# Third group's correlation in its own products, set-aside copies on GpSimd, last windows copied by ScalarE

## The chip, the cores and the metric

The kernel runs on one core of one Trainium2 chip. The metric is the device time of one execution in microseconds (us). The core has a matrix engine (TensorE, "PE" in the profile, with its weight loads listed apart as "PEld"), VectorE ("DVE"), ScalarE ("ACT"), GpSimd ("POOL"), and SyncE ("SP"), which here issues nearly all DMAs. Each engine works through its own instructions in order, and they wait for each other by semaphores.

## The reference

The input is a batch of 8 images with 768 channels of 32 x 32 pixels in float32. There are two layers, each with a residual:

```python
def _gn(v, G=32, eps=1e-5):
    g = v.reshape(B_, G, C_ // G, H_, W_)
    m = jnp.mean(g, axis=(2, 3, 4), keepdims=True)
    s = jnp.var(g, axis=(2, 3, 4), keepdims=True)
    return ((g - m) / jnp.sqrt(s + eps)).reshape(v.shape)
...
# layer 0: attention over 1024 tokens, 12 heads of 64; scores from variances of v and k
scores = var_v @ jnp.swapaxes(var_k, -2, -1) * scale
out = (softmax(scores) @ v) ... @ W_proj.T + b_proj
x = x + attention(_gn(x))
# layer 1: 1x1 convolution of the feature and of 28 correlation channels
feat_n = feature / norm
corr = [sum_c(feat_pad[:, :, r:h+r, cc:w+cc] * feat_n) for r, cc in offsets]   # 28 shifts
out = einsum('bchw,oc->bohw', concatenate([feature, corr]), conv_w) + conv_b
x = x + conv(_gn(x))
```

So the convolution has two parts: a 768 x 768 product over the 1024 pixels, and a product of the 28 correlation channels with a 768 x 28 matrix. The second is what the change moves.

## The kernel before, in words

**Products.** The large products (keys and values, projection "p", convolution "c") are done in seven block products instead of eight, numbered p = 1 to 7. For projection and convolution there are three groups g = 0, 1, 2. A group holds the output channel blocks g and g + 3, each 128 channels, for two token halves of 512 each. One block product is a "unit": three pairs of (128 x 128 weights, 128 x 512 operand), and `halves` (line 347) splits each pair into two matmul calls of 64 output columns. So a unit has six calls. In the trace each call is two records: the 3072 records of line 800 are 8 images x 6 head pairs x 8 tiles x 4 calls = 1536 calls. The products accumulate in a PSUM bank "x" (p = 1, 6, 7, 4 in turn), "y" (5, 3) or "z" (2). After p = 1, 5, 6 VectorE adds the partial sum to the output tile `acc`, and after p = 2, 3, 7, 4 one output block is final (`Wide.take`, line 1064).

**Correlation.** For each image `Corr` (line 1119) turns the image into blocks (`turn`), multiplies them on TensorE ("grams", `gram`, line 1138, 8 of them), copies each result out of PSUM into one of the `win` tiles, sends it to DRAM ("windowed"), reads diagonals back ("dd"), scales them, sends rows to DRAM and gathers them. `product` (line 1239) then forms the 28 rows of `cs` on VectorE. Three DMAs copy them to partitions 32, 64 and 96 (line 1243). The weights `wcorr_sb` are copied likewise (line 488).

**Where the correlation goes into the convolution.** `Conv.more` (line 1281) names the units whose bank is then final: p in (2, 3, 7, 4). Such a unit is begun but not closed (`Wide.unit`, line 1038). Then `join` (line 1053) issues one matmul of 28 rows x 128 columns for each held unit, each on its own quarter of the partitions. Images 0 to 5 join first four, four (groups 0 and 1), then two and two (group 2). Image 6 joins by two throughout, six times. Image 7 has `apart`: 12 correlation products in banks of their own, two for each of six `corr` calls (line 1337), added by VectorE.

**The order of the work.** The emitter keeps a model clock (`Clock`, line 92) with a cost for each unit (`T_US`, `CORR_US`, `STEP_US`). It decides with it in what order instructions go onto each engine's list; the engines then run by semaphores alone. `work_off` (line 1374) mixes the units in `rest` with the attention of the next image, four steps of products at a time, each step needing two exponentials from ScalarE. If only work of cost 0 is left in `rest`, `work_off` passes time until attention is done (`TAIL`, line 1383). The conv of image b runs beside the attention of image b + 1. `project` (line 1397) follows.

**The end.** Image 6's units (0, 2) and (1, 2) are held back into image 7's projection (line 1452), so that TensorE has work while image 7 is normalised. Their operands and outputs are copied aside first: `set_aside` (line 1315), five ScalarE copies of 128 x 512 into three tiles of the exponentials' pool `expool` (six tiles). It stands before the last three units of `rest` for image 6. Then the last iteration runs two units of image 7's convolution, the 8 grams, 16 more units, and three times two `corr` calls and a unit.

**The start.** `keep_warm(WARM)` issues 31 small matmuls while the first image loads.

**Queues.** SP issues the weight loads of the units (line 337, seven tiles ahead), the image loads and stores, and all small transfers of the correlation, in emission order. An SP instruction whose tile is not free holds those behind it.

Of the kernel before, what the change touches and what calls it, by code (L numbers as in the profile page):

```python
# [8 lines left out]
ALU = mybir.AluOpType  # L9
# [4 lines left out]
P = 128  # L14
NB, C, H, W = 8, 768, 32, 32
N = H * W
J = C // P
# [33 lines left out]
KVBLOCKS = 5  # L51
TBLOCKS = 7
HELD = 12
TAIL = 0.0
EXP, SUM, STEP_US = 1.07, 1.15, 1.73
KV_US, T_US, CORR_US = 1.93, 2.58, 1.2
GRAM_US = 1.4
WARM, BRIDGE = 31, (3, 7)

# [19 lines left out]

def conv_order(b):

    return QUADS if b < NB - 2 else (PAIR[:-2] if b == NB - 2 else PAIR) + SINGLE


def windows(ap, *dims):
# [85 lines left out]
def two_layers(ctx, tc, x, wkv, wproj, bproj, wconv, wcorr, bconv, out):  # L173
# [301 lines left out]
    def load_corr_weights():  # L475

        zero = cs[0:NROW, 0, 0:PAD]
        for r in rows:
            nc.sync.dma_start(out=r[:, 0:PAD], in_=zero)
            nc.sync.dma_start(out=r[:, PAD + N : ROW], in_=zero)  # L480
        for line, step in enumerate(STEP):
            for j in (1, 2, 3):
                n, k = CHANNELS.index(step * j), 3 * line + j - 1
                nc.sync.dma_start(out=wcorr_sb[n : n + 1, :, :], in_=wcorr[k : k + 1, :, :])
                nc.sync.dma_start(out=wcorr_sb[NS + n : NS + n + 1, :, :], in_=wcorr[NS + k : NS + k + 1, :, :])
        nc.sync.dma_start(out=wcorr_sb[2 * NS : NCH, :, :], in_=wcorr[2 * NS : NCH, :, :])
        for n in range(1, 4):
            nc.sync.dma_start(out=wcorr_sb[n * FOUR : n * FOUR + NCH, :, :], in_=wcorr_sb[0:NCH, :, :])

    later.after(130.0, mask_rows)  # L490
    later.after(150.0, load_corr_weights)
# [445 lines left out]
    class Attention:  # L937
# [32 lines left out]
        def exp_work(self, pair, t):  # L970
            def may():
                if ("c", 1) not in pair.rows_at or self.made - self.done >= AHEAD or self.made - self.summed > LAG:
                    return None
                free = self.free_at[self.made - AHEAD] if self.made >= AHEAD else 0.0
                return max(pair.rows_at["c", 1], free)

            def job():
                pair.exponentials(t)
                self.made += 1
                self.exp_at = clock.act  # L980

            clock.act_work(2 * EXP, may, job)
# [46 lines left out]
    class Wide:  # L1029
# [8 lines left out]
        def unit(self, g, p, between=None):  # L1038
            w = t_stream.take(self.kind, g, p)
            pairs = [(w[:, k, :], self.operand(p, k)) for k in range(JH)]  # L1040
            taken = lambda ps: self.take(g, p, ps)
            more = self.more(g, p) if self.more else None
            if more is None:
                banks.product(g, p, T_US, HF, pairs, taken, self.home if g == 2 else None)
            else:
                apart = (g, p) == (0, 2) and self.joined[:1] == [4]
                self.held.append((*banks.begin(g, p, HF, pairs, stop=False, between=between, apart=apart), taken, *more))
                if len(self.held) == (self.joined[0] if self.joined else 2):
                    self.joined = self.joined[1:]
                    self.join()  # L1050
            t_stream.fill()
# [67 lines left out]
    class Corr:  # L1119
# [18 lines left out]
        def gram(self, t):  # L1138

            b = self.b  # L1140
            tall = min(TALL, H - 4 * t)
            n = tall * WIDE
            if t not in self.turned:
                self.turn(t)
            block = self.turned[t]
            ps = other([P, SPAN], f"gr{b}_{t}")
            for j in range(J):
                image = self.f[:, j, :].rearrange("p (y x) -> p y x", x=W)
                for side in range(2):
                    left = side * (HW - 3)  # L1150
                    nc.tensor.matmul(  # L1151
                        ps[side * HD : (side + 1) * HD, :n].rearrange("p (y x) -> p y x", x=WIDE),
                        lhsT=block[:, j, side, :],
                        rhs=image[:, 4 * t : 4 * t + tall, left : left + WIDE],
                        start=j == 0, stop=j == J - 1,
                    )
            for ahead in range(t + 1, min(t + (3 if b == NB - 1 else 2), MT)):
                if ahead not in self.turned:
                    self.turn(ahead)

            def out():
                win = wins[t % 2 if t < MT - 1 else 2]
                vector.tensor_copy(win[:, :n], ps[:, :n])
                for side in range(2):
                    to = windowed[b % 2][t : t + 1, side * (HD * PITCH + HD - 3) :]
                    nc.sync.dma_start(
                        out=windows(to, (HW * PITCH - 3, 4), (PITCH, HW), (1, WIN)), in_=win[side * HD : (side + 1) * HD, :]
                    )
                if t % 4 == 3:
                    later.after(4.0, lambda: self.diagonals(t // 4))  # L1170

            later.after(GRAM_US + 0.25, out)
# [50 lines left out]
        def gather(self):  # L1223
# [19 lines left out]
                    nc.sync.dma_start(out=cs[n * FOUR : n * FOUR + NCH, :, :], in_=cs[0:NCH, :, :])  # L1243
                later.after_dve(6.0, lambda: ready.add(("cs", b)))

            later.after(18.0, product)

    class Conv:


        def __init__(self, b, f, acc, after):
            self.b, self.f, self.acc, self.after = b, f, acc, after
            self.early, self.then = False, None
            self.turn = False
# [12 lines left out]
        def start(self):  # L1267
# [9 lines left out]
            self.wide.joined = [4, 4] if self.b < NB - 2 else []  # L1277
            ready.add(("acc", self.b))
            later.after(7.0, self.thirds)

        def more(self, g, p):


            if p not in (2, 3, 7, 4) or self.apart:
                return None
            return g + JH * (p in (7, 4)), {2: 0, 3: 1, 7: 1, 4: 2}[p]

# [7 lines left out]
            ready.add(("fourth", self.b))  # L1295

        def units(self):
            b, held, sizes = self.b, 0, [4, 4] if self.b < NB - 2 else []
            need = {7: (("third", b),), 4: (("fourth", b),)}
            out = []  # L1300
            for g, p in conv_order(b):
                keys, us = need.get(p, ()), T_US
                if self.more(g, p):
# [27 lines left out]

        def corr_units(self):
            return [
                (CORR_US, (("cs", self.b),), lambda n=n: self.corr(self.apart[n : n + 2])) for n in range(0, len(self.apart), 2)
            ]

        def corr(self, parts):

            self.turn = not self.turn
            av = None if self.turn else two_banks(f"av{self.b}_{parts[0][0]}")  # L1340
            for n, (i, hf) in enumerate(parts):
                at = slice(n * FOUR, n * FOUR + NCH)
                ps = other([P, HF], f"cc{self.b}_{i}_{hf}") if av is None else av[n]
# [30 lines left out]
    def work_off(rest, attention=None, beside=()):  # L1374
        while rest or (attention and not attention.over()):
            if attention and not attention.over():
                clock.feed_act()
                if attention.can_run():
                    next_to(beside)
                    attention.run()  # L1380
                    next_to(beside)
                    continue
                if ("v", attention.b, 1) in ready and sum(r[0] for r in rest) <= TAIL:
                    clock.pass_time(0.5)
                    continue
            if rest and ready.issuperset(rest[0][1]):
                us, _, unit = rest.pop(0)
# [130 lines left out]
    for b in range(NB + 1):  # L1518
# [8 lines left out]
        if b:  # L1527
# [17 lines left out]
            if b < NB:  # L1545
# [69 lines left out]
```

## Time and profile before

| what | us |
|---|---|
| runs of before | 2604.48, 2602.58, 2604.71 (median 2604.48) |
| the profiled execution | 2601.92 |
| its span in the profile | 2599.4 |
| outside the span | 2.5 |
| TensorE busy | 2586.6 (100% of the span) |
| VectorE, ScalarE, GpSimd busy | 1609.8, 1368.6, 416.0 |
| granted TensorE clock | 1.0 |

The page has shares of busy time, a row of 40 slices, and a chain followed back from the last instruction. The chain of waits says at each step what released the work. The timelines list merged runs of instructions of one engine: start, length, engine, line, operation, operands, count, and in brackets the idle time before it and who ended it. A table by windows gives the busy time of each engine within a stretch. Matmul ends are modelled, so rates of TensorE are read from starts.

### The profile page before, as it was taken

How to read it: one execution, taken by the hardware profiler on the slowest of the kernel's cores; microseconds unless marked ns; L12 is line 12 of the kernel's file. 1: busy time of each engine (PE TensorE's matmuls, PEld its weight loads, DVE VectorE, ACT ScalarE, POOL GpSimd, SP SyncE). 2: the span in 40 equal slices, each digit the busy share in tenths (PEclk: the TensorE clock that was granted, in tenths of full speed). 3: DMA queues.
4: the chain of work that ended last, by engine and by line, in shares of the span. 5: the costliest groups of instructions: out<-in, count | busy, mean ns of one | idle time of the engine just before them, and what ended most of it. 6: DMA issues, size and time to landing. Idle time of an engine off the chain costs nothing.

```text
span 2599.4 us, 40526 instructions
## 1 busy us (share of the span) xinstructions
PE 2586.6 (100%) x14776; PEld 1351.1 (52%) x14776; DVE 1609.8 (62%) x4118; ACT 1368.6 (53%) x1841; POOL 416.0 (16%) x444
## 2 busy tenths in 40 slices
PE   9999999999999999999999999999999999999999
PEld 5654465434664347643476435764356643575333
DVE  6868735775347853488535885357853578535764
ACT  1497179701797017970189701896018960199500
POOL 4320130004300043000330013300133001330000
PEclk9999999999999999999999999999999999999999
DMA  8866366355563655636556365463654636545323
GB/s 295 291 222 216 105 206 206 102 200 168 175 206 96 203 169 173 202 105 200 171 170 201 121 200 169 156 205 118 206 170 144 207 123 205 187 125 169 114 91 106
DMA packets 324716, 448.16 MB, mean 172 GB/s; under 512 B 59810, under 2 KB 245522, under 8 KB 324518
## 3 DMA queue, kind: packets, MB, share of 16 engines
q1 hardware_dynamic: 322454, 442.24, 53.0%
q10 hardware_dynamic: 2064, 3.34, 0.4%
q8 instruction: 117, 1.92, 0.3%
q14 instruction: 81, 0.66, 0.1%
HBM read 376.70 MB, written 64.40 MB: 170 GB/s over the span
## 4 chain that ended last, share of the span: by engine, by line
PE 96%; DVE 1%; DMA 1%; ACT 0%; issue 0%; POOL 0%; SPq 0%; DVEq 0%; ACTq 0%; POOLq 0%
PE x L350 34%; PE av L800 25%; PE y L350 17%; PE z L350 9%; PE own L350 5%; PE gr L1151 3%; PE den L831 1%; PE den L887 1%; PE y L1057 1%; PE z L1057 1%; ACT ex L774 0%; DMA bc<-vdr 0%; DVE acc L167 0%; DMA xn<-in_x_dram 0%; DVE bn L167 0%
## 5 line engine op out<-in xcount | busy, mean ns | idle before, releaser
L774 ACT ACTIVATE ex<-bc,nk 128x1024 f32<-128x1024 f32 x768 | 827.5, 1137 | 403.9 <-DMA bc<-vdr 206.1
L800 PE MATMUL av<-ex,v 128*64 128x512 f32 x3072 | 693.5, 593 | 1.2 <-ACT ex L774 1.1
L800 PEld LDWEIGHTS av<-ex,v 128*64 128x64 f32 x3072 | 332.2, 137 | 318.4 <-issue 199.3
L784 ACT ACTIVATE junk<-bk,vm 128x1024 bf16<-128x1024 f32 x368 | 420.4, 1142 | 28.8 <-DMA bk<-kdr 19.1
L167 DVE TENSOR_TENSOR acc<-acc,ex 128x1024 f32<-128x1024 f32 x300 | 345.2, 1211 | 0.8 <-ACT ex L774 0.8
L229 ACT COPY kp<-x 128x384 f32<-128x384 f32 x28 | 13.3, 478 | 524.1 <-PE x L350 515.4
L350 PE MATMUL y<-kv,s 128*64 128x384 f32 x1488 | 265.3, 487 | 0.3 <-POOL s L636 0.3
L350 PE MATMUL x<-kv,xn 128*64 128x384 f32 x1512 | 259.5, 486 | 0.0
L350 PE MATMUL x<-kv,s 128*64 128x384 f32 x1488 | 256.4, 486 | 0.0
L350 PEld LDWEIGHTS x<-kv,xn 128*64 128x64 f32 x1512 | 139.5, 137 | 104.0 <-issue 83.8
L350 PEld LDWEIGHTS x<-kv,s 128*64 128x64 f32 x1488 | 142.6, 137 | 93.3 <-issue 72.7
L350 PEld LDWEIGHTS y<-kv,s 128*64 128x64 f32 x1488 | 137.0, 137 | 89.9 <-issue 72.4
L530 POOL TENSOR_TENSOR rstda<-vea,neghalf 128x1 f32<-128x1 f32 x8 | 4.8, 595 | 958.6 <-DVE vea L167 958.6
L1136 POOL TENSOR_TENSOR turn<-f,ones 128x384 f32<-128x384 f32 x112 | 110.9, 1010 | 242.7 <-PE gr L1151 165.7
L350 PE MATMUL z<-kv,xn 128*64 128x384 f32 x768 | 133.7, 486 | 0.0
L350 PE MATMUL x<-f,wt 128*64 128x512 f32 x504 | 118.3, 592 | 0.0
L167 DVE TENSOR_TENSOR v<-y,v 128x128 f32<-128x128 f32 x180 | 40.9, 282 | 122.2 <-PE y L350 122.2
L636 POOL TENSOR_TENSOR s<-xn 128x384 f32<-128x384 f32 x64 | 65.6, 1035 | 304.3 <-PE x L350 190.0
L167 DVE BATCH_NORM_STATS2 vbn<-v 128x6 f32<-128x64 f32 x720 | 101.6, 209 | 0.0
L350 PEld LDWEIGHTS z<-kv,xn 128*64 128x64 f32 x768 | 74.9, 137 | 47.3 <-issue 36.6
L167 DVE SCALAR_TENSOR_TENSOR xn<-x,bconv_sb,xn 128x512 f32<-128x512 f32 x63 | 46.3, 745 | 80.8 <-PE x L350 79.7
L1151 PEld LDWEIGHTS gr<-f,turn 128*64 128x64 f32 x1344 | 87.8, 136 | 13.0 <-issue 4.8
(202 smaller groups left out, 3132.3 us busy)
## 6 DMA issues: line engine op xcount, KB each, us to landing
kv<-kvs SPq DMA_DIRECT2D x124, 576.0 KB
kv<-in_wkv_dram SPq DMA_DIRECT2D x95, 576.0 KB
bc<-vdr SPq DMA_DIRECT2D x96, 512.0 KB
f<-in_x_dram SPq DMA_DIRECT2D x48, 512.0 KB
bk<-kdr SPq DMA_DIRECT2D x46, 512.0 KB
x1d<-f SPq DMA_DIRECT2D x42, 512.0 KB
xn<-x1d SPq DMA_DIRECT2D x42, 512.0 KB
out_dram<-xn SPq DMA_DIRECT2D x82, 256.0 KB
```

What stands on the lines that cost most here:

```text
L167: return getattr(self.engine, name)(*args, **kw)
L229: nc.scalar.copy(to, at)
L350: nc.tensor.matmul(out[at], lhsT=lhsT[:, at], rhs=rhs, start=start, stop=stop, **kw)
L636: nc.gpsimd.tensor_tensor(self.sums[g][:, 0], a[g][2], a[g][3], ALU.add)
L774: nc.scalar.activation(ex, self.bc[e], AF.Exp, scale=self.kv.nk[self.half][:, h, t : t + 1])
L784: nc.scalar.activation(junk, self.bk[e], AF.Exp, scale=self.kv.m2[self.half][:, h, t : t + 1], accum_out=self.sums[:, e, t : t + 1],)
L800: nc.tensor.matmul(self.av[hf][e * HD : (e + 1) * HD, :], lhsT=self.vt[:, t, e, :], rhs=exs[e][:, hf * HF : (hf + 1) * HF], start=t == 0, ...
L831: nc.tensor.matmul(den[at * 32 : (at + 1) * 32, :], lhsT=ones[:, 0:32], rhs=self.acc[e][:, hf * HF : (hf + 1) * HF], start=True, stop=True,)
L887: nc.tensor.matmul(den[e * HD : (e + 1) * HD, :], lhsT=ones, rhs=self.acc[e][:, at], start=True, stop=True)
L1057: nc.tensor.matmul(t, lhsT=wcorr_sb[at, i, :], rhs=cs[at, tokens, :], start=False, stop=True, skip_group_check=True)
L1136: nc.gpsimd.tensor_tensor(to[:, :, side], half, windows(ones, ones.ap[0], (0, J), (HW, 4), (1, HW)), ALU.mult)
L1151: nc.tensor.matmul(ps[side * HD : (side + 1) * HD, :n].rearrange("p (y x) -> p y x", x=WIDE), lhsT=block[:, j, side, :], rhs=image[:, 4 * ...
```

## The change

- Units of group 2 take their correlation as a fourth pair within their own product: all 128 rows of `wcorr_sb` and of `cs`, through `halves`. For this the weights of blocks 2 and 5 are no longer copied to the other three quarters (rows 28 and up of these two blocks stay zero); the copies of the rest take six DMAs instead of three.
- Image 6 joins once four (groups 0 and 1), then two, then (in the projection) two; its order has the units (2, 5) and (2, 1) between the pairs. Image 7's `apart` has 8 parts instead of 12, four for each of two `corr` calls, and its last four units follow them. In the order of the emission the correlation must be there one unit earlier.
- `set_aside` copies on GpSimd (multiplication by ones) and stands at the end of `rest`, after all exponentials of image 7 have been emitted. `TAIL` goes.
- Image 7's window copies move from VectorE to ScalarE, and its `product` is emitted 12 us of model time after the gather instead of 18.
- 42 small matmuls at the start instead of 31.

```diff
-TAIL = 0.0
-KV_US, T_US, CORR_US = 1.93, 2.58, 1.2
+KV_US, T_US, CORR_US, OWN_US = 1.93, 2.58, 1.2, 0.43
-WARM, BRIDGE = 31, (3, 7)
+WARM, BRIDGE = 42, (3, 7)
...
-    return QUADS if b < NB - 2 else (PAIR[:-2] if b == NB - 2 else PAIR) + SINGLE
+    if b < NB - 2:
+        return QUADS
+    if b == NB - 2:
+        return PAIR[:10] + ((2, 5),) + PAIR[10:12] + ((2, 1),) + SINGLE[2:]
+    return PAIR + SINGLE
...
         for n in range(1, 4):
-            nc.sync.dma_start(out=wcorr_sb[n * FOUR : n * FOUR + NCH, :, :], in_=wcorr_sb[0:NCH, :, :])
+            for g in range(0, J, JH):
+                at = slice(g, g + JH - 1)
+                nc.sync.dma_start(out=wcorr_sb[n * FOUR : n * FOUR + NCH, at, :], in_=wcorr_sb[0:NCH, at, :])
...
                 self.made += 1
+                if self.made == HP * MT:
+                    ready.add(("made", self.b))
...
-            if more is None:
+            if more and g == JH - 1:
+                i, tokens = more
+                pairs.append((wcorr_sb[:, i, :], cs[:, tokens, :]))
+                banks.product(g, p, T_US + OWN_US, HF, pairs, taken)
+            elif more is None:
...
-                vector.tensor_copy(win[:, :n], ps[:, :n])
+                if b < NB - 1:
+                    vector.tensor_copy(win[:, :n], ps[:, :n])
+                else:
+                    act_copy(0.3, win[:, :n], ps[:, :n])
...
-            later.after(18.0, product)
+            later.after(18.0 if b < NB - 1 else 12.0, product)
...
-            self.apart = [] if b < NB - 1 else [(i, hf) for i in (0, 3, 1, 4, 2, 5) for hf in range(2)]
+            self.apart = [] if b < NB - 1 else [(i, hf) for i in (0, 3, 1, 4) for hf in range(2)]
+        def sizes(self):
+            return [4, 4] if self.b < NB - 2 else [4]
...
-            if p not in (2, 3, 7, 4) or self.apart:
+            if p not in (2, 3, 7, 4) or (self.apart and g < JH - 1):
                 return None
...
+            def copy(to, at):
+                one = windows(ones, ones.ap[0], (0, HF // HD), (1, HD))
+                to, at = [a.rearrange("p (n d) -> p n d", d=HD) for a in (to, at)]
+                nc.gpsimd.tensor_tensor(to, at, one, ALU.mult)
             for k in range(JH):
-                act_copy(0.55, self.high[k], self.f[:, JH + k, :HF])
+                copy(self.high[k], self.f[:, JH + k, :HF])
             for g in range(2):
-                act_copy(0.55, self.low[g], self.acc[:, g, :HF])
+                copy(self.low[g], self.acc[:, g, :HF])
...
-            self.turn = not self.turn
-            av = None if self.turn else two_banks(f"av{self.b}_{parts[0][0]}")
-            for n, (i, hf) in enumerate(parts):
+            some = [other([P, HF], f"cc{self.b}_{i}_{hf}") for i, hf in parts[:2]]
+            for n, (ps, (i, hf)) in enumerate(zip(some + two_banks(f"av{self.b}_{parts[0][0]}"), parts)):
...
-                if ("v", attention.b, 1) in ready and sum(r[0] for r in rest) <= TAIL:
-                    clock.pass_time(0.5)
-                    continue
...
-                    rest.insert(len(rest) - 3, (0.0, (), conv.set_aside))
+                    rest.append((0.0, (("made", b),), conv.set_aside))
             else:
                 units, parts = conv.units(), conv.corr_units()
-                rest += [first, start] + units[:2] + grams + units[2:18]
-                for n, unit in enumerate(units[18:]):
-                    rest += parts[2 * n : 2 * n + 2] + [unit]
+                rest += [first, start] + units[:2] + grams + units[2:17]
+                for n, unit in enumerate(units[17:]):
+                    rest += parts[n : n + 1] + [unit]
```

More of the change, by code (lines that the diff above doesn't have):

```diff
@@ L1253, in __init__ @@
             self.early, self.then = False, None
-            self.turn = False
-            self.apart = [] if b < NB - 1 else [(i, hf) for i in (0, 3, 1, 4, 2, 5) for hf in range(2)]
+            self.apart = [] if b < NB - 1 else [(i, hf) for i in (0, 3, 1, 4) for hf in range(2)]
             self.parts = {(i, hf, "f") for i in range(J) for hf in range(2)} | {(*q, "c") for q in self.apart}
             self.sums = TokenSums(f"f{b}", [f[:, k, :] for k in range(JH)], [f[:, JH + k, :] for k in range(JH)])
+        def sizes(self):
+            return [4, 4] if self.b < NB - 2 else [4]
         def residual(self, n):
@@ L1276, in start @@
             )
-            self.wide.joined = [4, 4] if self.b < NB - 2 else []
+            self.wide.joined = self.sizes()
             ready.add(("acc", self.b))
@@ L1297, in units @@
         def units(self):
-            b, held, sizes = self.b, 0, [4, 4] if self.b < NB - 2 else []
+            b, held, sizes = self.b, 0, self.sizes()
             need = {7: (("third", b),), 4: (("fourth", b),)}
@@ L1302, in units @@
                 keys, us = need.get(p, ()), T_US
-                if self.more(g, p):
+                if self.more(g, p) and g == JH - 1:
+                    keys, us = keys + (("cs", b),), us + OWN_US
+                elif self.more(g, p):
                     keys, held = keys + (("cs", b),), held + 1
@@ L1333, in corr_units @@
             return [
-                (CORR_US, (("cs", self.b),), lambda n=n: self.corr(self.apart[n : n + 2])) for n in range(0, len(self.apart), 2)
+                (CORR_US, (("cs", self.b),), lambda n=n: self.corr(self.apart[n : n + 4])) for n in range(0, len(self.apart), 4)
             ]
         def corr(self, parts):
-            self.turn = not self.turn
-            av = None if self.turn else two_banks(f"av{self.b}_{parts[0][0]}")
-            for n, (i, hf) in enumerate(parts):
+            some = [other([P, HF], f"cc{self.b}_{i}_{hf}") for i, hf in parts[:2]]
+            for n, (ps, (i, hf)) in enumerate(zip(some + two_banks(f"av{self.b}_{parts[0][0]}"), parts)):
                 at = slice(n * FOUR, n * FOUR + NCH)
-                ps = other([P, HF], f"cc{self.b}_{i}_{hf}") if av is None else av[n]
                 nc.tensor.matmul(ps, lhsT=wcorr_sb[at, i, :], rhs=cs[at, hf, :], start=True, stop=True)
```

## The prediction

> **What bounds the kernel.** I read the page's busy shares first, then the chain of waits, then the table by windows.
>
> ```profile
> PE 2586.6 (100%) x14776; PEld 1351.1 (52%) x14776; DVE 1609.8 (62%) x4118; ACT 1368.6 (53%) x1841; POOL 416.0 (16%) x444
> ...
> PE 96%; DVE 1%; DMA 1%; ACT 0%; issue 0%; POOL 0%; SPq 0%; DVEq 0%; ACTq 0%; POOLq 0%
> ```
>
> ```profile
> 606.00:926.00 320.00, 320.00 (x1838) 164.46 (x1836) 194.39 (x506) 172.07 (x234) 51.23 (x54) 1.00 0.53 170
> ...
> 2520.00:2540.00 20.00, 17.98 (x224) 12.51 (x224) 15.24 (x29) 7.10 (x16) 0.00 (x0) 1.00 0.24 76
> 2540.00:2600.00 60.00, 55.52 (x258) 21.23 (x254) 24.84 (x47) 0.00 (x0) 2.03 (x2) 1.00 0.38 110
> ```
>
> The columns are window, length, then busy time (instructions) of TensorE, its weight loads, VectorE, ScalarE, GpSimd, then clock, DMA share and GB/s. One image takes about 320 us, and in it TensorE has no gap. So in the middle of the run only TensorE's own work counts: each microsecond added there is added to the time, and no other engine can give one back. Gaps are at the ends only: the span less TensorE's busy time is 12.8 us, and a few more hide inside merged runs.
>
> **The joins (images 0 to 5).** I take the price of a join from starts in the chain of waits. First two held units of group 2, then four held units:
>
> ```profile
> 842.09 2.58 PE x L350 x12
> 844.66 0.62 PE y L1057
> 845.29 0.01 PE x L1057
> 845.29 0.42 PE y L1057
> 845.72 0.01 PE x L1057
> 845.72 7.02 PE av L800 x32
> ```
>
> ```profile
> 779.68 2.58 PE y L350 x12
> 782.25 0.62 PE y L1057
> ...
> 783.32 0.01 PE y L1057
> 783.32 2.73 PE z L350 x12
> ```
>
> A join of two takes from 844.66 to 845.72, 1.06 us, and the run of products behind it lasts 7.02 where undisturbed ones last 6.87: 0.15 more. A join of two costs 1.21 us. A join of four takes 782.25 to 783.32, 1.07, and the unit behind it 2.73 against 2.58: 1.22 us. So the price does not depend on how many are joined.
>
> The change replaces two joins of two (2.42 us) by four extra pairs in units. A unit of three pairs is 12 records in 2.577 us (two units, 24 records, stand at 5.15), so a pair (two calls, four records) is 0.859 us, of the same shape 128 x 64 by 128 x 512 as its neighbours. Four pairs cost 3.43 us. That is **1.02 us more for each image, and 6.1 us for images 0 to 5**, on the path. (The emitter's own constant for the pair is 0.43 us, half of it; that is a rival below.) The weight loads of the pair are hidden as all others are: PEld is busy 52%. Units of group 2 are now evicted at once instead of after the join, which helps VectorE, but nobody waits for it there: 0.
>
> **Image 6.** Before its projection it has five joins of two, 6.05 us. Afterwards one join of four, one of two, and four pairs: 1.22 + 1.21 + 3.43 = 5.86. **-0.2 us.** The join in the projection stays. New is that (2, 5) follows the join of four and needs the y bank of (0, 3), which VectorE has first to add out: 0.69 us, up to 1.2 more if one of attention's additions is ahead. Where four steps of attention (6.87 us) come between, as they did behind the old join at 2385.75, it is hidden. Bounds 0 and 2; I take **+0.5**, since the model clock may choose either.
>
> **Image 7.** From 2581.09, where its first correlation product starts, to the last product's end at 2595.55 are 14.46 us. Less three units (7.73), the six calls of `corr` cost 6.73. Afterwards two joins of four and four pairs, 2.44 + 3.43 = 5.87: **-0.9 us** (0.5 of it is a late arrival of the correlation rows, which may come back, see below).
>
> **Set-aside to GpSimd, at the end.** ScalarE's and TensorE's timelines:
>
> ```profile
> 2440.86 1.65 ACT L229 COPY held<-f 128x512 f32<-128x512 f32 x3
> 2447.36 1.14 ACT L229 COPY held<-xn 128x512 f32<-128x512 f32 x2 [4.85 <-PE av L800]
> 2448.40 4.51 ACT L774 ACTIVATE ex<-bc,nk 128x1024 f32<-128x1024 f32 x4
> ```
>
> ```profile
> 2445.44 3.60 PE L800 MATMUL av<-ex,v 128*64 128x512 f32 x16
> 2449.60 3.15 PE L800 MATMUL av<-ex,v 128*64 128x512 f32 x10 [0.56 <-ACT ex L774]
> 2452.97 1.50 PE L800 MATMUL av<-ex,v 128*64 128x512 f32 x5 [0.22 <-ACT ex L774]
> ```
>
> The third set-aside tile is one of the exponentials' six. ScalarE stands 4.85 us until TensorE frees it, and the last four exponentials are queued behind. TensorE then waits for them. The unit before ends at 2445.61; four steps (6.87) and a unit (2.58) should end at 2455.06, and end at 2457.47. With the copies gone from ScalarE, two exponentials can run at 2441 to 2443 and two when tiles come free at 2447, before TensorE needs them. **-2.4 us**; bounds 0 (something else is late) and -2.6.
>
> On GpSimd a 128 x 384 multiplication by ones takes 1.01 us (other two-operand forms 0.99 to 2.12), so 512 columns 1.35, at worst 2.8, and five 6.8 to 14. They start once the tiles of steps 5 and 6 are free, about 2449, and end at 2456 to 2463. Behind them wait the loads of the new residual into `f` on SP (issued 2458 to 2466 before) and the held units at 2514. The loads need the first three copies only (2453, at worst 2457.5). So 0; without that cover SP would stop for 1 to 2 us, with weights loaded seven tiles ahead, still 0 on TensorE.
> The Trainium skill speaks against it: "GPSIMD Engine Reference", section 8, says that GpSimd shares its SBUF interfaces with VectorE and contends with VectorE instructions that have two SBUF inputs. In this trace all 200 additions of attention last 1.156 to 1.227 us, so no row shows that loss. If the four additions there doubled (4.8 us), VectorE would end them about 2457 instead of 2452, and the denominators' product, due at 2456, would come up to 1 us late.
>
> **Grams of image 7.** In VectorE's timeline:
>
> ```profile
> 2532.80 0.30 DVE L167 COPY win<-gr 128x133 f32<-128x133 f32 x1 [1.00 <-DMA windowed<-win]
> 2534.68 0.30 DVE L167 COPY win<-gr 128x133 f32<-128x133 f32 x1 [1.57 <-DMA windowed<-win]
> ```
>
> The first copy comes only at 2529.51, though gram 0 is done at 2527.5, since VectorE's own sums (1.9 us) are ahead. From copy to landed DMA are 2.9 us (2529.79 to 2532.69), and there are two tiles. The grams last 13.4 us (2526.06 to 2539.45) where seven at 1.42 and one of 1.0 make 10.9. On ScalarE the first copy can start at 2527.6 (about 0.27 us, from 0.57 for 512 columns and 0.48 for 384), between the turn copies (0.92 a gram, 1.2 with it, under 1.42). Following the ring from there, gram 5 waits 0.3 and gram 7 0.4: end 2537.8. **-1.6 us**; bounds 0 (the same DMAs hold ScalarE, with the turn copies queued behind it) and -2.4.
>
> **Correlation rows.** They are needed 15 units and two small transposes (38.7 + 0.44) after the grams: 2537.8 + 39.1 = 2576.9, where before it was 2581.1. VectorE formed them at 2576.64, placed by the model's 18 us; the last gather DMA was issued at 2566.18 and, by the 2.2 us of the window DMAs, landed about 2568.4. With 12 us the multiplication stands two evictions earlier, about 2569 to 2570 with the grams' gain. Multiplication and subtraction take 1.9, the three copies' issue 2.6, landing 2.2: 2576 to 2577. Just in time: **+0.2**.
>
> **Priced at 0.** Eleven more matmuls at the start: the last 15 records before the gap took 1.61 us, so 22 take 2.4, inside the 2.83 us that TensorE waits until 13.45 (bounds -0.2 and +0.3). Three more weight DMAs at 160 us (0.79 each): TensorE's recorded waits have none there; uncovered 2.4. Without `TAIL` the last four weight loads of image 0's projection go out about 15 us earlier, in a stretch of SP that is idle; else 2 us of SP.
>
> **Sum.** +6.1 - 0.2 + 0.5 - 0.9 - 2.4 - 1.6 + 0.2 = **+1.7 us**. Against the profiled execution (2601.92) that is 2603.6. The median of the runs is 2.6 higher, so I forecast 2604.5 + 1.7 = **2606.2**.
>
> **Rivals.**
> - *Rows late* (slower). If the VectorE multiplication keeps its old place, 2575 after the grams' gain, the copies land at 2581.7 and TensorE stands 4.8 us at 2576.9. That gives +6.3, 2610.8. It decides as soon as the multiplication starts after about 2570. For it: no slack in the sum above, and a gather that SP issues late (2561.28, behind weight loads that wait for tiles). Against: the 6 us.
> - *The ends give nothing back* (slower): ScalarE's order or the DMA ring keeps both stalls. +5.7, 2610.2. Against: the 4.85 us wait clearly has one cause.
> - *The pair costs 0.43* (the change is cheaper than it looks): -4.2, -1.9 and -2.6 for the three kinds of images, and -3.3: -12, 2592.5. Against: four records of 0.215 each everywhere.
>
> **Chances.** Forecast 0.65; late rows 0.17; nothing given back 0.13; pair at 0.43 0.05. A measurement can tell 0.2% (5.2 us) from no change. Both slower rivals stand near that line, so slower 0.23, same 0.71, faster 0.06. The range goes from all bounds of the gains together (0.0, less 2 us of scatter of the runs) to the slower rivals with 1 us more: 2602.3 to 2611.8.
>
> **What would show it.** Right: units of group 2 with 16 records in 3.43 us, no 1.06 us joins behind them, about 321.3 us an image; the run of products at 2445 unbroken; grams in about 11.8 us; the first join of image 7 starting right behind its unit. Wrong: 14 records, or a unit of 3.0 us; a wait for an exponential there; TensorE waiting for `cs`.

## The result and the profile after

| | runs | median, us | lowest to highest |
|---|---|---|---|
| before | 18 | 2602.94 | 2601.22 to 2604.71 |
| after | 18 | 2607.05 | 2605.65 to 2610.83 |

After / before is 1.0016, with a 95% interval of 1.0009 to 1.0024: 4.1 us longer, between about 2.3 and 6.2. The profiled execution of after took 2608.87, its span is 2607.2, and 1.7 lie outside it. It is 1.8 above its own median, while that of before is 1.0 below its median, so the two profiles differ by more (spans: 7.8 us) than the kernels do.

To see where the time comes from I cut both spans at the same events: the first record of each image's projection ("own"), the first gram of image 7, the first unit behind the grams, the end of the last product.

| stage | before | after | difference |
|---|---|---|---|
| start to image 0's mark | 271.43 | 272.15 | +0.7 |
| image 0 | 271.54 | 274.31 | +2.8 |
| images 1 to 5, each | 320.25 | 321.26 | +1.01, five times |
| image 6's mark to grams | 381.85 | 384.09 | +2.2 |
| grams to next unit | 13.19 | 11.25 | -1.9 |
| next unit to the last product's end | 56.3 | 55.4 | -0.9 |

TensorE is still the bound. The page's busy shares, then the same window in the middle as for before (window, length, busy time and instructions of TensorE, its weight loads, VectorE, ScalarE, GpSimd, then clock, DMA share, GB/s):

```profile
PE 2594.9 (100%) x14862; PEld 1416.7 (54%) x14862; DVE 1610.2 (62%) x4106; ACT 1368.3 (52%) x1844; POOL 427.8 (16%) x449
```

```profile
606.00:926.00 320.00, 320.00 (x1840) 184.11 (x1837) 193.62 (x506) 172.08 (x234) 50.03 (x54) 1.00 0.54 170
```

TensorE's busy time rose by 8.3 us, the span by 7.8, and the middle has no gap in either kernel. What the change did to an image stands in the chain of waits of after, at the end of image 1's convolution (start, length, engine, output, line, count):

```profile
526.14 2.58 PE x L353 x12
528.71 3.43 PE y L353 x16
532.15 1.72 PE den L892 x8
533.86 3.43 PE x L353 x16
537.30 3.43 PE z L353 x16
540.73 6.01 PE x L353 x28
```

Units of group 2 have 16 records in 3.43 us, where 12 took 2.58: three stand here by themselves, the fourth is merged with a unit of 12 in the last line (28 records, 6.01). The joins of line 1057 (now 1068) are gone from this place. Four times 0.86 against two joins: +1.0 us an image.

The end of attention over image 7 is where the forecast gain did not appear. The timelines of after, TensorE first, then VectorE, then GpSimd (in brackets: idle time before, and who ended it):

```profile
2456.41 7.04 PE L805 MATMUL av<-ex,v 128*64 128x512 f32 x32
...
2469.65 1.07 PE L892 MATMUL den<-acc,ones 128*64 128x512 f32 x2 [0.20 <-DVE acc L170]
...
2471.86 1.50 PE L892 MATMUL den<-acc,ones 128*64 128x512 f32 x5 [1.13 <-DVE acc L170]
```

```profile
2457.62 0.25 DVE L170 RECIPROCAL inv<-inv 128x16 f32<-128x16 f32 x1 [4.50 <-DMA inv<-den]
...
2460.60 11.20 DVE L170 TENSOR_TENSOR acc<-acc,ex 128x1024 f32<-128x1024 f32 x6
2471.73 2.96 DVE L170 TENSOR_TENSOR t1o<-v 128x512 f32<-128x512 f32 x3
```

```profile
2461.98 6.54 POOL L1341 TENSOR_TENSOR held<-f,ones 128x512 f32<-128x512 f32 x3 [103.12 <-DVE acc L170]
2468.48 4.46 POOL L1341 TENSOR_TENSOR held<-xn,ones 128x512 f32<-128x512 f32 x2
```

The run of 32 products is unbroken, so the wait for ScalarE is gone, as forecast. But while GpSimd multiplies (2462 to 2473), VectorE's six additions take 11.20 us: the first two 1.22 each, the four that run beside the multiplications 2.28 to 2.30. In before all 350 such additions (not 200, as the prediction counted) took 1.156 to 1.227. The denominators' product then waits 0.20 and 1.13 for them.

The second place is image 6's convolution, in TensorE's timeline of after:

```profile
2393.89 2.80 PE L353 MATMUL y<-t1f,wt 128*64 128x512 f32 x12 [0.77 <-DVE xn L170]
...
2424.68 3.08 PE L353 MATMUL x<-f,wt 128*64 128x512 f32 x12
2428.60 2.80 PE L353 MATMUL x<-t2f,wt 128*64 128x512 f32 x12 [0.84 <-DVE xn L170]
```

The first is unit (2, 5) behind the join of four. The last two are (2, 1) and (2, 6), which now follow each other directly and use the same bank x: VectorE has to add (2, 1) out first. What the two waits cost is read from starts. From the join's first start (2391.99) to the start of the products behind (2, 5) (2396.52) are 4.53 us, where a join of four (1.06) and the unit behind it (2.73) make 3.79: 0.74 lost. From the start of (2, 1) to that of the products behind (2, 6) (2431.23) are 6.55, where two units make 5.15: 1.40 lost. Together 2.1 us.

The grams of image 7, TensorE and ScalarE:

```profile
2536.87 7.08 PE L1162 MATMUL gr<-f_last,turn 128*64 128x133 f32 x120
...
2544.14 2.98 PE L1162 MATMUL gr<-f_last,turn 128*64 128x133 f32 x48 [0.18 <-ACT win L232]
2547.28 1.01 PE L1162 MATMUL gr<-f_last,turn 128*64 128x76 f32 x24 [0.16 <-ACT win L232]
```

```profile
2538.45 0.27 ACT L232 COPY win<-gr 128x133 f32<-128x133 f32 x1 [0.70 <-PE gr L1162]
```

The copy starts 1.58 us behind the first gram's start (in before 3.45), and two waits of 0.18 and 0.16 are all that is left. Last, the correlation rows: VectorE, the queue of SP, and their first use on TensorE.

```profile
2577.71 1.20 DVE L170 TENSOR_TENSOR cs<-cs,v 28x1024 f32<-28x1024 f32 x1
```

```profile
2580.23 2.57 SPq L1257 DMA_DIRECT2D cs<-cs  x3
```

```profile
2587.28 0.70 PE L1365 MATMUL cc<-cs,wcorr_sb 28*128 28x512 f32 x2
```

There is no wait in front of the first product. The three copies are issued by 2582.8. With a landing time of 2.2 us (that of the window DMAs) to 2.7 (that of the last copy in e7 below) they are there at 2585.0 to 2585.5, an estimate: about 2 us ahead of their use.

### The profile page after: what moved, and what is told of

Its sections match the earlier page's. It is cut to its first block, busy times and chain, and to the rows that moved or that the text cites. A ratio compares the mean times of both kernels' runs of the same rounds, so it can differ in the third digit from the quotient of the medians.

```text
span 2607.2 us, 40692 instructions
## 1 busy us (share of the span) xinstructions
PE 2594.9 (100%) x14862; PEld 1416.7 (54%) x14862; DVE 1610.2 (62%) x4106; ACT 1368.3 (52%) x1844; POOL 427.8 (16%) x449
## 4 chain that ended last, share of the span: by engine, by line
PE 97%; DMA 1%; DVE 1%; issue 1%; ACT 0%; SPq 0%; POOL 0%; ACTq 0%; DVEq 0%; POOLq 0%
PE x L353 35%; PE av L805 25%; PE y L353 18%; PE z L353 10%; PE own L353 5%; PE gr L1162 3%; PE den L836 1%; PE den L892 1%; DMA bc<-vdr 0%; DMA xn<-in_x_dram 0%; DVE acc L170 0%; ACT ex L779 0%; PE y L1068 0%; PE z L1068 0%; DMA windowed<-win 0%
## 5 line engine op out<-in xcount | busy, mean ns | idle before, releaser
L353 PEld LDWEIGHTS x<-kv,xn 128*64 128x64 f32 x1512 | 147.2, 137 | 96.2 <-issue 74.9
L353 PEld LDWEIGHTS x<-kv,s 128*64 128x64 f32 x1488 | 150.0, 137 | 86.8 <-issue 63.3
L353 PEld LDWEIGHTS y<-kv,s 128*64 128x64 f32 x1488 | 145.4, 137 | 81.7 <-issue 63.0
```

The lines of the kernel that those rows point to most:

```text
L353: nc.tensor.matmul(out[at], lhsT=lhsT[:, at], rhs=rhs, start=start, stop=stop, **kw)
```

## The experiments

The theory after the result: pairs +6.1; image 6's two stalls about +1.9; ScalarE's exponentials -2.4, of which GpSimd's copies give some back by slowing VectorE; grams -1.9; end -0.9. The rivals were: that the set-aside's contention costs nothing and the rest is scatter; that the three extra weight DMAs during image 0 cost some 1.7; that the pairs of images 0 to 5 are not what makes the kernel longer. Each kernel was timed beside before on one chip; e1 to e4 shared one chip, e5 to e8 another. Medians of before there: 2603.24 and 2603.05.

**e1: set aside on ScalarE, at the same late place.**

```diff
             def copy(to, at):
-                one = windows(ones, ones.ap[0], (0, HF // HD), (1, HD))
-                to, at = [a.rearrange("p (n d) -> p n d", d=HD) for a in (to, at)]
-                nc.gpsimd.tensor_tensor(to, at, one, ALU.mult)
+                act_copy(0.55, to, at)
```

> The changed kernel with the five set-aside copies on ScalarE instead of GpSimd, at the same late place. Theory: GpSimd's copies slow VectorE's additions beside them (1.87 us each in the changed kernel's profile against 1.21), and so the denominators' product comes about 2.8 us late. Then the additions are back at 1.21, TensorE no longer waits for them at the end of image 7's attention, and the time falls by 2.8 us from 2607.0 to about 2604.2. Rival: the additions are late because the late exponentials are; then TensorE waits as before and the time stays at 2607.

Measured: 2605.83, ratio 1.0011 (1.0003 to 1.0020). VectorE's timeline of e1, and TensorE's behind it:

```profile
2460.55 6.89 DVE L170 TENSOR_TENSOR acc<-acc,ex 128x1024 f32<-128x1024 f32 x6
2467.36 1.89 DVE L170 TENSOR_TENSOR t1o<-v 128x512 f32<-128x512 f32 x3
```

```profile
2470.43 1.89 PE L892 MATMUL den<-acc,ones 128*64 128x512 f32 x8
```

With the copies on ScalarE the same six additions take 6.89 us instead of 11.20, the three sums 1.89 instead of 2.96, and the denominators' product has no wait. So GpSimd's copies are what slows VectorE. The stage from image 6's mark to the grams is 381.61 instead of 384.09. The gain in the median is 1.2 us, though, and not the 2.8 that was expected: the profile of after shows the contention at its worst. A difference of 1.2 is little more than the scatter of the runs, so the cause rests on the rows and not on the times. In four other kernels with these copies the stage takes 382.01 (e2), 383.01 (e4), 382.98 (e6) and 383.09 (e7); with after's the mean is 383.0. All five have the same four additions of 2.28 to 2.30; e4, e6 and e7 have a wait of 0.45 to 0.54 for them. In e2 VectorE comes out of its DMA wait in front of the reciprocal after 2.40 us instead of 4.50, and there the product does not wait at all. So the price of the copies is 0.4 to 2.5, on average 1.4 us. The stage also holds image 6's grams, which wait for GpSimd's `turn` copies in some profiles and not in others (0.32 us recorded in e8, none in e5), so a few tenths of these figures are not the set-aside's.

**e3: the same copies on GpSimd, with one operand.**

```diff
-                one = windows(ones, ones.ap[0], (0, HF // HD), (1, HD))
-                to, at = [a.rearrange("p (n d) -> p n d", d=HD) for a in (to, at)]
-                nc.gpsimd.tensor_tensor(to, at, one, ALU.mult)
+                nc.gpsimd.tensor_copy(to, at)
```

> The changed kernel with GpSimd's plain copy instead of the multiplication by ones, at the same place. Theory A: what slows both engines is the sum of their reads; with one operand instead of two the copies take about half (1.1 us instead of 2.2), the additions beside them are slowed for half the time, and about 1.4 us come back: 2605.6. Theory B: any GpSimd access slows an addition of two SBUF operands as much as the other would; then additions beside the copies still take 1.8 us, but fewer of them, and 0.5 to 2 us come back. If the copies are as long as before, nothing does: 2607.

Measured: 2605.99, ratio 1.0012 (1.0003 to 1.0021). GpSimd, then VectorE, of e3:

```profile
2459.80 4.38 POOL L1339 COPY held<-f 128x512 f32<-128x512 f32 x3 [101.22 <-PE av L805]
2464.13 3.15 POOL L1339 COPY held<-xn 128x512 f32<-128x512 f32 x2
```

```profile
2458.26 8.54 DVE L170 TENSOR_TENSOR acc<-acc,ex 128x1024 f32<-128x1024 f32 x6
```

A copy takes 1.46 to 1.58 us, the multiplication by ones 2.2; the six additions stretch to 8.54, between e1 and after, and the four beside the copies take 1.62 to 1.63 each. Neither theory's numbers are met (copies of 1.1, additions of 1.8), but with one operand both engines lose less than with two, as theory A has it. The time is that of e1 (0.2 more, less than the runs differ).

The loss could have been read in the trace of before, from other work of the same two engines. GpSimd and VectorE of before, near the start (the last line is the same VectorE work with GpSimd idle):

```profile
20.46 1.96 POOL L638 TENSOR_TENSOR s<-s,xn 128x384 f32<-128x384 f32 x2
22.38 4.20 POOL L640 TENSOR_TENSOR s<-xn,s 128x384 f32<-128x384 f32 x2
```

```profile
21.91 7.96 DVE L167 TENSOR_TENSOR ws<-ws 128x1152 f32<-128x1152 f32 x4 [3.23 <-DMA ws<-in_wkv_dram]
52.52 3.90 DVE L167 TENSOR_TENSOR ws<-ws 128x1152 f32<-128x1152 f32 x3 [1.44 <-DMA ws<-in_wkv_dram]
```

VectorE's operations here, with both operands in SBUF, take 7.96 / 4 = 1.99 us each beside GpSimd's two-operand ones and 3.90 / 3 = 1.30 without. GpSimd's own go from 0.98 to 2.10 as soon as VectorE's begin. Record by record, of the sixteen VectorE operations of this shape the eight that start beside a GpSimd operation take 1.73 to 2.15 us, the other eight 1.34 to 1.36.

**e2: images 0 to 5 join group 2 by two, as in before.** The rest of the change stays, but the weight copies are three DMAs again. The blocks 2 and 5 of the copied quarters are set to zero when image 6 begins.

```diff
-            if more and g == JH - 1:
+            if more and g == JH - 1 and self.own:
...
+            self.wide.own = self.b >= NB - 2
+            if self.b == NB - 2:
+                for n in range(1, 4):
+                    for i in (JH - 1, J - 1):
+                        nc.gpsimd.memset(wcorr_sb[n * FOUR : (n + 1) * FOUR, i, :], 0.0)
...
-                if self.more(g, p) and g == JH - 1:
+                if self.more(g, p) and g == JH - 1 and self.b >= NB - 2:
```

> The changed kernel, but images 0 to 5 join group 2 by two as in the kernel before, and only images 6 and 7 have the fourth pair. The weight copies at the start are three DMAs again; the quarters that must be zero for the pairs are cleared by small GpSimd memsets when image 6's convolution starts. Theory: the pairs cost 1.02 us an image, and the three extra weight DMAs 0.7 us in image 0: the time falls by 6.8 us to about 2600.2, and images 1 to 5 take 320.25 us each instead of 321.27. Rival: the loss has other sources (order, late exponentials of image 1), and the time falls by less than 3 us.

Measured: 2599.6, ratio 0.9987 (0.9978 to 0.9995): some 7.5 less than after, and 3.6 less than before. Images 1 to 5 take 320.25 each again. The chain of waits of e2, at the place shown of after:

```profile
529.83 2.58 PE x L353 x12
532.40 0.62 PE y L1066
...
533.46 2.73 PE z L353 x12
```

The join of 1.06 us is back, and units have 12 records. This settles the largest term: the pairs of images 0 to 5 cost the 6 us, and without them the rest of the change is a gain.

**e4: the weight copies as a job of their own, later in the run.** The profile of after has image 0 1.75 us longer than its pairs explain, and six weight-copy DMAs hold SP for 4.88 us there instead of 2.52 for three.

```diff
+    def copy_corr_weights():
         for n in range(1, 4):
             for g in range(0, J, JH):
...
+    later.after(230.0, copy_corr_weights)
```

> The changed kernel with the six DMAs that copy the correlation weights to the other quarters issued some 80 us of model time later. Theory: in the changed kernel's profile image 0's projection starts 0.7 us later than before, because the three extra DMAs hold the SP queue 2.4 us longer just ahead of key and value weights; moved, the start is back at 271.4 us and the time falls by 0.7 us to 2606.3. Rival: the later landing of image 1's first rows (2.3 us late, 1.8 us lost) hangs on the same queue; then it falls by up to 2.5. If both are scatter of single executions, 0.

Measured: 2607.0, ratio 1.0016 (1.0008 to 1.0025), the time of after: the expected fall of 0.7 did not come. Most of the extra 1.75 us is scatter: the stretch up to image 1's mark, less 1.02 where the kernel has pairs, takes 542.97 in the profile of before, 545.44 in after's, 542.75 in e4's (the code of after but for that job) and 542.37 (e2) to 546.30 (e1) in the others. It is not short wherever there are three copies again (e8 545.03, e9 544.43), and where it is long, the profiled execution lies above its own median, as after's does. The +0.7 and the 1.75 of the first table belong there; what a part of them might be owed to is below what these runs resolve.

**e5: image 6 in its old order, on top of e1.** Its groups 0 and 1 join by two again; the pairs of group 2 stay.

```diff
-        return PAIR[:10] + ((2, 5),) + PAIR[10:12] + ((2, 1),) + SINGLE[2:]
+        return PAIR[:-2] + SINGLE
...
-            return [4, 4] if self.b < NB - 2 else [4]
+            return [4, 4] if self.b < NB - 2 else []
```

> The changed kernel with the set-aside copies on ScalarE, and image 6 in the order of the kernel before, its groups 0 and 1 joined by two. Theory: in the changed kernel TensorE waits twice for VectorE in image 6, 0.76 us at (2, 5) and 0.84 at (2, 6), with their restarts about 1.9 us; two more joins of two instead of one of four cost 1.2. Without the stalls the stretch from image 6's projection to image 7's grams, 381.6 us with ScalarE's copies and the new order, falls by 0.7 to 380.9, and the time from 2605.8 to 2605.1. Rival: the stalls are hidden elsewhere (the attention's exponentials would be waited for instead), and it rises by the 1.2 us.

Measured: 2604.34, ratio 1.0006 (0.9997 to 1.0015). From 2300 to 2520 us TensorE waits for nothing. The stage takes 380.45 against e1's 381.61, though TensorE has 1.2 us more work in it (three joins of two, 3.63, instead of 1.22 + 1.21). So the two stalls with what follows them cost 1.2 + 1.2 = 2.4 us; e8, which has the same products in the same order here, takes 381.00, and by it they cost 1.8. The 2.1 read from after's timeline lies between. And 380.45 is 381.85 + 1.0 (3.63 + 3.43 against the old five joins, 6.05) - 2.4: the forecast gain from the exponentials is there in full, once nothing takes it back. e9 below shows it by itself: its image 6 has the units and joins of before, only the set-aside is late, and the stage takes 379.43, 2.4 less than in before.

**e6: window copies of image 7 on VectorE, as before.**

```diff
-                if b < NB - 1:
-                    vector.tensor_copy(win[:, :n], ps[:, :n])
-                else:
-                    act_copy(0.3, win[:, :n], ps[:, :n])
+                vector.tensor_copy(win[:, :n], ps[:, :n])
```

> The changed kernel with image 7's window copies on VectorE again. Theory: from the first gram to the unit behind the last one it took 13.2 us with VectorE and 11.25 with ScalarE, since VectorE's sums stand before the first copies; the stretch goes back to 13.2, and the time rises by 1.9 us from 2607.0 to 2609.0. Rival: the two window tiles and their DMAs set the pace of the grams, and the stretch stays at 11.3.

Measured: 2608.97, ratio 1.0023 (1.0013 to 1.0032). From the first gram to the next unit are 13.24 us, as in before. TensorE's timeline of e6 shows one of the four waits for `win` that are back:

```profile
2539.34 1.58 PE L1162 MATMUL gr<-f_last,turn 128*64 128x133 f32 x24 [0.97 <-DVE win L170]
```

**e7: the rows of image 7 at the old 18 us of model time.** This tests the rival of late rows: does the 12 decide?

```diff
-            later.after(18.0 if b < NB - 1 else 12.0, product)
+            later.after(18.0, product)
```

> The changed kernel with the correlation rows of image 7 formed 18 us of model time after the gather, as before, instead of 12. Theory: in the changed kernel VectorE forms them at 2577.7, the copies are issued until 2582.8 and needed at 2587.3. Two evictions later they are issued until about 2590.7 and land near 2593, and TensorE stands about 5.5 us at the first join of image 7: 2612.5. Rival: the gather lands so late that the place of the multiplication does not decide, and the time stays at 2607.

Measured: 2614.71, ratio 1.0047 (1.0033 to 1.0060): 7.7 us more than after. TensorE's timeline of e7, and its windows (columns as above):

```profile
2589.34 1.12 PE L1365 MATMUL cc<-cs,wcorr_sb 28*128 28x512 f32 x2 [1.96 <-DMA cs<-cs]
...
2591.76 2.07 PE L1365 MATMUL av<-cs,wcorr_sb 28*128 28x512 f32 x2 [0.20 <-DMA cs<-cs]
2593.76 4.86 PE L353 MATMUL y<-f_last,wt 128*64 128x512 f32 x12
```

```profile
2588.00:2590.00 2.00, 0.66 (x2) 0.29 (x2) 0.11 (x1) 0.00 (x0) 0.00 (x0) 1.00 0.90 197
2590.00:2592.00 2.00, 1.80 (x5) 0.53 (x4) 1.09 (x2) 0.00 (x0) 0.00 (x0) 0.78 0.66 174
2592.00:2594.00 2.00, 2.00 (x4) 0.50 (x6) 0.42 (x2) 0.00 (x0) 0.00 (x0) 0.50 0.68 262
...
2596.00:2598.00 2.00, 2.00 (x6) 0.47 (x4) 0.00 (x0) 0.00 (x0) 0.00 (x0) 0.51 0.04 14
2598.00:2600.00 2.00, 2.00 (x16) 0.59 (x12) 0.47 (x1) 0.00 (x0) 0.00 (x0) 1.00 0.00 0
```

The rival's mechanism exists and the 12 takes it away. The expected time was 2612.5. The first of the call's four products starts at 2586.26 and the unit behind them at 2593.76, 7.5 us for what takes 1.07 in after. And the wait costs more than itself: TensorE, busy for 0.66 of 2 us from 2588, has a granted clock of 0.78 from 2590 and of 0.50 from 2592, full again only from 2598, and the unit in between takes 4.86 us instead of 2.80.

**e8: e2, e1 and e5 together.** Joins by two for images 0 to 5, set-aside on ScalarE, image 6 in its old order.

> Three edits together: images 0 to 5 join group 2 by two again, the set-aside copies are on ScalarE, and image 6 has the order and the joins by two of the kernel before; the rest of the change stays (fourth pair in images 6 and 7, windows by ScalarE, rows at 12 us, set-aside at the end). If the single effects add up: 2599.6 measured with the joins alone, less 1.3 for the copies, less 0.7 for image 6: 2597.6, ratio to before 0.9978. Rival: the copies' gain and image 6's gain are of the same slack, and it stays at 2598.5 or above.

Measured: 2597.85, ratio 0.9981 (0.9972 to 0.9989). The single effects add up to within 0.3 us (2597.6 expected); the rival's 2598.5 is only 0.65 away, so it is made unlikely rather than ruled out.

**e9: no pairs at all.** As e8, with joins of two in image 6 and 12 correlation products of image 7 in three calls of four. Copies by ScalarE, the late place of the set-aside and the 12 us stay.

```diff
-            if more and g == JH - 1:
-                i, tokens = more
-                pairs.append((wcorr_sb[:, i, :], cs[:, tokens, :]))
-                banks.product(g, p, T_US + OWN_US, HF, pairs, taken)
-            elif more is None:
+            if more is None:
...
-            self.apart = [] if b < NB - 1 else [(i, hf) for i in (0, 3, 1, 4) for hf in range(2)]
+            self.apart = [] if b < NB - 1 else [(i, hf) for i in (0, 3, 1, 4, 2, 5) for hf in range(2)]
...
-            return [4, 4] if self.b < NB - 2 else [4]
+            return [4, 4] if self.b < NB - 2 else []
```

> No fourth pairs at all: images 0 to 6 join group 2 by two, and image 7 has 12 separate correlation products in three calls of four; images 0 to 6 as in the kernel before, set-aside copies on ScalarE at the end, windows on ScalarE, rows at 12 us. Theory: a join costs 1.2 us whatever it joins, a pair 0.86. Against the three edits together, image 6 saves 3.43 - 2.42 = 1.0 and image 7 3.43 - 1.22 = 2.2 us: 2597.85 - 3.2 = 2594.6, ratio to before about 0.9968. Rival: VectorE's four additions after each call (2.6 us) hold the banks that the next call needs and the last units' evictions, and less than 1.5 us come back: 2596.4 or more.

Measured: 2594.2 (2594.01 to 2595.3), ratio 0.9966 (0.9952 to 0.9979) against 2602.73 for before on that chip: 8.5 us less, the best version of all, as expected (2594.6) and clear of the rival's 2596.4. So VectorE's four additions behind each call hold nothing up. One of its calls of four, in the chain of waits of e9:

```profile
2575.76 0.63 PE cc L1355 x2
...
2576.83 2.73 PE y L353 x12
```

Four products of the correlation take 2576.83 - 2575.76 = 1.07 us, with 0.15 on the unit behind them (2.73); as pairs they are 3.43.

## Why the prediction was nearly right, and where it failed

The time on record, 2606.2, is 0.85 below the measured 2607.05, and "no change that can be told" is what came. Part of that is luck. The forecast stood on a median of 2604.48 from three runs; 18 runs give 2602.94. On that base +1.7 makes 2604.6, and the measured change is +4.1: it was 2.4 us too small.

| step | forecast | measured | by |
|---|---|---|---|
| pairs, images 0 to 5 | +6.1 | +6.1 (1.01 each in the profile) | marks, e2 |
| image 6: work | -0.2 | not separable | |
| image 6: stalls | +0.5, bounds 0 and 2 | +2.1 (1.8 to 2.4) | timeline, e5, e8 |
| set-aside: exponentials no longer late | -2.4 | -2.4 | e9, e5 |
| set-aside: GpSimd's copies | 0 | +1.4 (0.4 to 2.5) | e1 |
| grams | -1.6 | -1.9 | marks, e6 |
| image 7's end | -0.9 | -0.9 | marks |
| rows just in time | +0.2 | 0 | timeline, e7 |

The stage from image 6's mark to the grams, 383.0 on average against 381.85, is +1.2, where the forecast had -0.2 + 0.5 - 2.4 = -2.1. With +6.1 - 1.9 - 0.9 that makes +4.5, against 4.1 in the medians, within their interval. So two terms of the sum failed, each by 1.4 to 1.6 us: the cost of GpSimd's copies, put at 0, and image 6's stalls, put at 0.5. The grams gave 0.3 more than forecast and the rows cost 0.2 less. The lower end of the range, 2602.3, is 0.2 below what its own working gives (2604.5 + 0.0 - 2).

- **Pairs: right.** The price from merged records (0.859 us) held to a hundredth, and so did "the price of a join does not depend on how many are joined". The rival at 0.43 is refuted by the 3.43 us of a unit with 16 records. Nothing hides there, because TensorE has no gap in an image.
- **Image 6: the mechanism was right, the size was not.** "(2, 5) follows the join of four and needs the y bank" was one stall of the two, and I took +0.5, hoping that steps of attention would come between. None came. The second stall I missed: the new order puts (2, 6) directly behind (2, 1), on the same bank. The order in the diff shows it without any trace.
- **Set-aside: the step that failed.** "So 0", since "no row shows that loss". That reading was wrong. No addition of attention in before runs beside a two-operand GpSimd operation, so those rows could not show it; the rows of `ws` could, and do (1.99 against 1.30, shown under e3). The "0.99 to 2.12" quoted for GpSimd's two-operand forms is the same thing seen from the other side: the 2.1 stand beside such VectorE work. The prediction wrote the loss down, as denominators "up to 1 us late" if the additions doubled, but with no term in the sum. They nearly doubled (2.29 against 1.22), the product waited 1.33 us in after's profile, and the copies' price was 1.4 on average and 2.5 in the profile. The copies also took 2.2 us each, within the bounds (1.35 to 2.8) and far from the 1.35 chosen. The Trainium skill, "GPSIMD Engine Reference", section 8, says that GpSimd shares SBUF interfaces with VectorE and contends with VectorE instructions that have two SBUF inputs. The runs agree: 2.29 us an addition beside GpSimd's multiplications against 1.22 without.
- **Rows late: rejected, rightly.** They came about 2 us early. e7 has the rival's case, at 7.7 us more than after, where I had priced the standing at 4.8: the fall of the clock was missing from the price, and the standing itself was 6.4.
- **Ends give nothing back: refuted**, by grams, image 7's end and e5.
- **Priced at 0:** the longer warm-up costs nothing (TensorE's first product starts at 16.51 against 16.50; the wait in the gap falls from 2.83 to 0.28). For the weight DMAs e4 shows no cost. `TAIL` was not tried by itself.

## What to carry to other kernels

Where TensorE has no gap, compare the two forms of a small product by the time between starts: here a few matmuls of 28 rows on separate quarters cost 1.07 us, two as well as four, a full pair of 128 rows 0.86 each, so joining wins from two up. Before work goes to an idle GpSimd, look at what VectorE does in the same stretch and who waits for VectorE next; an empty engine is not a free one. "No row shows the loss" holds only if the two engines run beside each other in some row with the same kind of operands; look for such rows in any shape and at any place of the trace. When an order of units is rewritten, go through it bank by bank: each unit that follows another on the same bank waits for the eviction, unless something stands between.

## What the runs showed of the hardware

- Additions of VectorE (128 x 1024, both operands in SBUF) took 2.28 to 2.30 us each beside GpSimd multiplications with two operands, 1.62 to 1.63 beside GpSimd copies with one operand, and 1.22 beside ScalarE's copies. GpSimd's multiplication of 128 x 512 took 2.2 us there; its copy 1.46 to 1.58.
- In e7 TensorE's late rows lowered its clock: 0.50 and 0.51 under full load from 2592 to 2598, after windows in which it was busy for 0.66 and 1.80 of 2 us. Of the lost time 6.4 us lie before the unit (7.5 - 1.07) and 2.1 in it (4.86 - 2.80); that is 8.5 in this profile, whose execution lies 1.65 above the median. The Trainium skill, "TensorE: Matmul & The Clock Gate", Part 1, says that TensorE's clock falls to half after an idle window of about 3.4 us. The half agrees with this trace. The length does not show in it: the recorded idle stretches are 1.96 and 0.20 us, and between them TensorE was at work.
- Single executions of one kernel spread over 3.5 to 5 us. In the profiles, one for each kernel, most of this lies in the first 550 us (542.4 to 546.3 to image 1's mark). Between kernels with the same units, images 1 to 4 repeat to 0.01 us and image 5 to 0.17. The stage of images 6 and 7 moves by half a us between e5 and e8, which have the same products in the same order there.
